# Two graph convolutions in one kernel: the groups of spans counted from the end, so that the last group is whole and serves block 48 alone

## The chip, the cores and the metric

The kernel runs on one core of a Trainium2 chip. The metric is device time in microseconds of one execution. The kernel before took 2149.52 us (median of 3 runs, 2146.58 to 2150.33).

Engines are named as in the profile: PE is TensorE, DVE is VectorE, ACT is ScalarE, POOL is GpSimd, SP is SyncE. PE multiplies, POOL issues the gathers (indirect DMAs, one row of 512 floats for each of 128 partitions), SP issues the plain DMAs, DVE and ACT do the elementwise work and take results out of PSUM.

## The reference

A graph of 6250 nodes and 100000 edges, sorted by destination; 512 features a node, all in float32. Cut to what matters:

```python
h = relu(layernorm(x))
dinv = where(deg > 0, rsqrt(max(deg, 1)), 0)          # deg counts src
norm = -dinv[src] * dinv[dst]
def conv(x, W0, W1, b):
    tx1 = segment_sum(x[src] * norm[:, None], dst)      # the propagation
    return x @ W0 + tx1 @ W1 + b
h = layer_norm(conv(h, W1_0, W1_1, b1)) * gamma + beta
h = where(h >= 0, h, 0.01 * h)
return x + conv(h, W2_0, W2_1, b2)
```

So there are two layers. Each gathers 100000 rows of 2 KB (x[src]), sums them by destination node, and multiplies 6250 x 512 by two 512 x 512 matrices. The second layer's gathers read what the first layer has written, from any node.

## The kernel before, in words

**Units of work.** The nodes are 49 *blocks* of 128 (block 48 has 106). The edges are 782 *chunks* of 128 in order of destination. A gather (L382, in `gather_to`) fetches one chunk, 128 rows, into one of 57 slots of the tile `places`, which are used in turn. A *span* (in the code a unit, `NU` = 261 of them) is a run of 32 consecutive nodes, of which it uses the first ones: span u begins at the node where chunk 3u begins, about 24 nodes after the span before it, and sums chunks 3u to 3u+3. Four spans make a *group*, 66 groups (`NS`). Before the change, groups are counted from the front: group g has spans 4g to 4g+3, and the last group, 65, has one span with two chunks, 780 and 781.

**What is done with a group.** `sums(g)` first builds `sel` on DVE (L465 and L474): for each span and chunk a 128 x 32 matrix of ones where an edge belongs to a node of the span. Then each product (L480) multiplies such a matrix by a gathered chunk and adds into one of four column quarters of the array, `ps[q * 32 : q * 32 + 32]`: quarter q holds span q of the group. The loop's outer index is the chunk's place in the span (`SPAN` = 4), the inner one the span, so that neighbouring products are in different quarters. ACT takes the 128 x 512 result out of PSUM as `agg[g]` (L483).

**What is done with a block.** A block is *due* when the last group that overlaps it is complete. `inside[i]` lists the groups that may overlap block i, with a margin of `DRIFT` = 32 nodes on either side for the uncertainty of where a group begins. Then:

- `turn(layer, i)` issues SP's loads for block i+2, transposes the block's own rows (`own`, L451, result taken out by ACT at L453), and *places* the groups' sums (`place`): for each group in `inside[i]`, DVE builds a 0/1 matrix `there` (L493) and PE does four products (L496) that both transpose the sums and shift them to the block's nodes. DVE scales the result into `aT` (L548).
- `dense(layer, i, ...)` multiplies the transposed own rows by W0 and `aT` by W1 (L458, four products each), and `finish` does the rest on DVE and ACT: in layer 0 bias (L511), layer norm, leaky relu, and two stores, to `tab[1]` (L527, which layer 1 gathers from) and `h_tab` (L532); in layer 1 bias (L506), the addition of x (L507) and the store of the output.

**Order.** PE, POOL and SP execute in the order in which the code issues (`manual_schedule`); DVE and ACT are put in order by a scheduler. For each layer the loop runs over the groups g: issue gathers as far as slots allow; `turn` for each block that is due (its last group is before g); `sums(g)`; then `dense` for those blocks. At g = NS - 2, the last group but one, the code does not wait for the next round: it does every block that doesn't need the last group (`turn` and `dense` of block 47), then for block 48 everything that can be done without the last group: its own transposes, its first products, and the placement of all its groups but the last. Then comes `sums(65)`, the last placement, the second products of block 48 and `finish`.

**Start.** Before the first group, the kernel computes degrees, the statistics of the first layer norm, the table of normalised rows (`make_table`, stored to `tab[0]`) and, for the first 60 chunks, which are gathered from x directly, scales each row after the gather (`find`, `look_up`, L407, L422 and L433). L326 spreads the first node of each span over the partitions (`row_ps`), from which `node_of` comes (L334 to L336).

**Check.** At g = 33 of layer 0, `check` counts violations of what the layout assumes: that the edges are sorted, that no span covers more than 32 nodes, and that each group begins within `DRIFT` nodes of its mean place. If the count is not zero, a second, general algorithm runs after this one.

Of the kernel before, what the change touches and what calls it, by code (L numbers as in the profile page):

```python
# [12 lines left out]
OP = mybir.AluOpType  # L13
# [6 lines left out]
P = 128  # L20
# [4 lines left out]
Q = 32  # L25
NQ = P // Q
STEP = 3
SPAN = STEP + 1
DRIFT = 32
# [10 lines left out]
def gnn_kernel(  # L40
# [45 lines left out]
    NS = -(-NU // NQ)  # L86
    rows = [min(P, N - i * P) for i in range(NB)]
# [216 lines left out]
    with tc.tile_pool(name="turn", bufs=1) as wp, tc.tile_pool(  # L304
# [18 lines left out]
        for k in range(2):  # L323
            for q in range(NQ):
                at = STEP * (q + k)
                nc.tensor.matmul(row_ps[q * Q : (q + 1) * Q, k, :], last.to_broadcast([P, Q]),  # L326
                                 dlx[:, at : at + STEP * NQ * (NS - 1) + 1 : STEP * NQ], start=True, stop=True)
# [27 lines left out]
def usual_path(tc, have):  # L355
    nc = tc.nc
    (x, out, tab, h_tab, ndinv_d, sidx, dlx, iota_r, w_sb, W2_1, W2_0, w_late, ident, eps, ones, first, node_of, minus,
     unsorted, ln, dinv, sdinv, bias1, bias2, gam, bet, unseen, N, E, D, NB, NC, NU, NS, KD, rows, places, order,
     groups, xs, sc, pick, src_lo, src_hi, p_id, dup) = (
        have[n] for n in ("x out tab h_tab ndinv_d sidx dlx iota_r w_sb W2_1 W2_0 w_late ident eps ones first node_of "  # L360
                          "minus unsorted ln dinv sdinv bias1 bias2 gam bet unseen N E D NB NC NU NS KD rows places "
# [4 lines left out]
    GN = NQ * STEP * P * N / E  # L366
    inside = [range(max(0, math.floor((i * P - DRIFT) / GN)), min(NS, math.ceil((i * P + r + DRIFT) / GN)))
              for i, r in enumerate(rows)]
    with ExitStack() as es:
# [6 lines left out]
        def zr(t):  # L376
            return places[:, order[t % R], :]
# [83 lines left out]
        def sums(g):  # L461

            n = min(NQ, NU - NQ * g)
            node = pool.tile([P, NQ, Q], F32, name="node")
            nc.vector.tensor_tensor(node[:, :n, :], first[:, NQ * g : NQ * g + n, None].to_broadcast([P, n, Q]),  # L465
                                    iota_r[:, None, 1 : Q + 1].to_broadcast([P, n, Q]), op=OP.add)
            sel = pool.tile([P, NQ, SPAN, Q], F32, name="sel")
            chunk = [range(STEP * (NQ * g + q), min(STEP * (NQ * g + q) + SPAN, NC)) for q in range(n)]
            same = n if len(chunk[-1]) == SPAN else 1
            for q in range(0, n, same):  # L470
                w = len(chunk[q])
                of = dlx[:, 1 + chunk[q][0] : 2 + chunk[q][0]]
                of = bass.AP(tensor=of.tensor, offset=of.offset, ap=[of.ap[0], [STEP, same], [1, w], [0, Q]])
                nc.vector.tensor_tensor(sel[:, q : q + same, :w, :], of,  # L474
                                        node[:, q : q + same, None, :].to_broadcast([P, same, w, Q]), op=OP.is_equal)
            ps = psum.tile([P, D], F32, name="ps")
            for s in range(SPAN):
                for q in range(n):
                    if s < len(chunk[q]):
# [508 lines left out]
```

## Time and profile before

| what | value |
|---|---|
| median of 3 runs (lowest, highest) | 2149.52 us (2146.58, 2150.33) |
| profiled execution, its own time | 2148.89 us |
| its span, first to last instruction | 2146.7 us |
| PE, POOL busy | 84%, 71% |
| DVE, ACT busy | 31%, 18% |
| granted PE clock, mean | 0.926 |
| DMA | 527.05 MB, 246 GB/s over the span |
| gathers from the tables (L382) | 1504, 0.96 us each |
| layer 0's last gather issued | 1087.69 us |
| layer 1's first gather issued | 1123.74 us |
| layer 1's last gather issued | 2109.66 us |

A row of the costliest groups gives the line, the engine, the operation, tiles, shape and count, then the busy time in us and the mean of one in ns, and after the second bar the engine's idle time before these instructions and what ended most of it. A row of the timeline gives start and duration in us, engine, line and operation; "x24" says that 24 records that follow each other are shown as one, and the bracket gives the idle time before them. A product in float32 leaves two records on PE (two passes), so the four products of one placement are 8 passes. A row of the windows gives, for one stretch of time, its length and then busy time and count for PE, the weight loads, DVE, ACT and POOL, the granted clock, the DMA engines' share and GB/s.

### The profile page before, as it was taken

Reading aid. Unit: us, or ns where it says so; the run is one execution under the profiler, and the core shown is the slowest. Engines: PE = TensorE matmul, PEld = TensorE weight load, DVE = VectorE, ACT = ScalarE, POOL = GpSimd, SP = SyncE. Lnnn points to the kernel's source line nnn. Section 1 sums busy time; section 2 is a strip of 40 time slices with the busy share of each in tenths; the row PEclk is TensorE's granted clock in tenths of the full one; section 3 lists DMA queues with packets and bytes.
Section 4 is the critical chain, followed back from the end, with each engine's and each line's share of the span. In section 5 each row is a group of like instructions: output and inputs, shape, how many; then the busy total and the mean of one; then the engine's idle time right before and its main releaser. Section 6 shows DMA issues by size and latency. Waiting matters only on the chain.

```text
span 2146.7 us, 23527 instructions
## 1 busy us (share of the span) xinstructions
PE 1795.7 (84%) x8843; PEld 794.7 (37%) x8843; DVE 674.8 (31%) x1341; ACT 382.7 (18%) x694; POOL 1520.2 (71%) x1577
## 2 busy tenths in 40 slices
PE   5669888988879888988876888889888888889888
PEld 4534333333334333433331333334333333334333
DVE  8974323333334233333330212212212212211211
ACT  7774212111112122111110000000000000000000
POOL 5067777777777777777727777777777777777772
PEclk9779999999989999999997989999999999999989
DMA  9298888788788888788837788888878888877883
GB/s 368 82 354 264 247 254 254 242 250 255 243 286 249 253 255 250 240 255 244 254 121 229 243 251 256 255 251 245 256 243 255 243 251 257 256 248 247 245 252 117
DMA packets 198945, 527.05 MB, mean 246 GB/s; under 512 B 31864, under 2 KB 46019, under 8 KB 198822
## 3 DMA queue, kind: packets, MB, share of 16 engines
q0 software_dynamic: 125120, 410.09, 62.4%
q1 hardware_dynamic: 73702, 115.36, 15.5%
q8 instruction: 71, 1.16, 0.2%
q14 instruction: 52, 0.43, 0.1%
HBM read 474.06 MB, written 51.27 MB: 245 GB/s over the span
## 4 chain that ended last, share of the span: by engine, by line
PE 48%; DMA 29%; POOL 9%; issue 8%; DVE 5%; ACT 0%; POOLq 0%; SPq 0%; ACTq 0%; DVEq 0%
DMA places<-tab,sidx 28%; PE u_ps L458 25%; PE ps L480 15%; POOL places L382 9%; PE aT_ps L496 5%; PE hT_ps L451 1%; DVE hi L252 1%; DVE lo L252 1%; DVE places L393 0%; PE both_ps L258 0%; DMA places<-in_x_dram,sidx 0%; DVE places L394 0%; PE u_ps L422 0%; PE hT_ps L422 0%; DVE both L428 0%
## 5 line engine op out<-in xcount | busy, mean ns | idle before, releaser
L382 POOL DMA_INDIRECT places<-tab,sidx x1504 | 1444.5, 960 | 493.8 <-issue 315.8
L480 PE MATMUL ps<-places,sel 128*32 128x512 f32 x4168 | 732.4, 666 | 280.7 <-DMA places<-tab,sidx 268.1
L480 PEld LDWEIGHTS ps<-places,sel 128*32 128x32 f32 x4168 | 141.8, 117 | 781.0 <-DMA places<-tab,sidx 591.3
L474 DVE TENSOR_TENSOR sel<-dlx,node 128x512 f32<-128x512 f32 x132 | 90.9, 688 | 750.0 <-PE ps L480 750.0
L496 PE MATMUL aT_ps<-there,agg 128*128 128x128 f32 (+2 forms) x2080 | 253.8, 278 | 1.4 <-ACT agg L483 1.4
L496 PEld LDWEIGHTS aT_ps<-there,agg 128*128 128x128 f32 (+1 forms) x2080 | 246.1, 196 | 4.2 <-ACT agg L483 3.2
L483 ACT ACTIVATE agg<-ps 128x512 f32<-128x512 f32 x132 | 78.8, 597 | 918.9 <-PE ps L480 918.9
L458 PE MATMUL u_ps<-places,hT 128*128 128x512 f32 (+1 forms) x392 | 185.8, 618 | 0.7 <-ACT hT L453 0.7
L458 PE MATMUL u_ps<-w,hT 128*128 128x512 f32 (+1 forms) x392 | 181.1, 605 | 0.7 <-ACT hT L453 0.7
L458 PE MATMUL u_ps<-places,aT 128*128 128x512 f32 (+1 forms) x392 | 178.0, 597 | 0.7 <-DVE aT L548 0.7
L458 PE MATMUL u_ps<-w,aT 128*128 128x512 f32 (+1 forms) x392 | 176.3, 592 | 0.7 <-DVE aT L548 0.7
L506 DVE TENSOR_TENSOR u_ps<-u_ps,bias 128x512 f32<-128x512 f32 x48 | 33.6, 700 | 294.9 <-PE u_ps L458 294.9
L511 DVE TENSOR_TENSOR u_ps<-u_ps,bias 128x512 f32<-128x512 f32 (+1 forms) x49 | 34.3, 700 | 284.3 <-PE u_ps L458 284.3
L453 ACT ACTIVATE hT<-hT_ps 128x512 f32<-128x512 f32 (+1 forms) x98 | 58.3, 595 | 349.6 <-PE hT_ps L451 348.2
L458 PEld LDWEIGHTS u_ps<-places,hT 128*128 128x128 f32 (+1 forms) x392 | 72.3, 195 | 117.3 <-issue 116.5
L458 PEld LDWEIGHTS u_ps<-w,hT 128*128 128x128 f32 (+1 forms) x392 | 70.3, 189 | 109.0 <-issue 106.5
L458 PEld LDWEIGHTS u_ps<-places,aT 128*128 128x128 f32 (+1 forms) x392 | 74.8, 191 | 95.4 <-issue 94.6
L458 PEld LDWEIGHTS u_ps<-w,aT 128*128 128x128 f32 (+1 forms) x392 | 74.3, 190 | 94.3 <-issue 93.4
L382 POOL DMA_INDIRECT places<-in_x_dram,sidx x44 | 45.0, 1024 | 86.8 <-ACT places L396 57.7
L448 ACT ACTIVATE h<-h,ln 128x512 f32<-128x512 f32 (+1 forms) x49 | 39.7, 813 | 283.3 <-DMA h<-in_x_dram 283.3
L493 DVE TENSOR_SCALAR there<-iota_r,node_of 128x128 f32<-128x128 f32 x260 | 76.6, 295 | 38.7 <-PE aT_ps L496 38.6
L548 DVE TENSOR_TENSOR aT<-aT_ps,to 128x512 f32<-128x512 f32 (+1 forms) x98 | 67.1, 685 | 39.4 <-PE aT_ps L496 37.9
(128 smaller groups left out, 942.7 us busy)
## 6 DMA issues: line engine op xcount, KB each, us to landing
places<-tab,sidx POOLq DMA_INDIRECT x1504
h<-in_x_dram SPq DMA_DIRECT2D x48, 256.0 KB
tab<-t SPq DMA_DIRECT2D x48, 256.0 KB
h_tab<-g SPq DMA_DIRECT2D x48, 256.0 KB
h<-h_tab SPq DMA_DIRECT2D x48, 256.0 KB
xt<-in_x_dram SPq DMA_DIRECT2D x48, 256.0 KB
out_dram<-t SPq DMA_DIRECT2D x48, 256.0 KB
places<-in_x_dram SPq DMA_DIRECT2D x4, 1792.0 KB
```

The costliest lines, as they stand in the source:

```text
L252: nc.vector.tensor_tensor(t, s[:, g * 2 * GJ : (g + 1) * 2 * GJ].rearrange("p (j s) -> p j s", s=2)[:, :, None, :] .to_broadcast([EP, GJ, ...
L382: nc.gpsimd.indirect_dma_start(out=zr(t), out_offset=None, in_=x if layer == 0 and t < RAW else tab[layer], in_offset=bass.IndirectOffsetO ...
L448: nc.scalar.activation(h[:r], h[:r], AF.Relu, bias=ln[:r, 1, i : i + 1], scale=ln[:r, 0, i : i + 1])
L453: nc.scalar.activation(hT[:, :, :r], ps[:, :, :r], AF.Copy)
L458: nc.tensor.matmul(u_ps[:r], hT[:, kc, :r], w[:, kc, :], start=(start and kc == 0), stop=(not start and kc == KD - 1))
L474: nc.vector.tensor_tensor(sel[:, q : q + same, :w, :], of, node[:, q : q + same, None, :].to_broadcast([P, same, w, Q]), op=OP.is_equal)
L480: nc.tensor.matmul(ps[q * Q : (q + 1) * Q, :], sel[:, q, s, :], zr(chunk[q][s]), start=(s == 0), stop=(s == len(chunk[q]) - 1))
L483: nc.scalar.activation(agg[g][: n * Q], ps[: n * Q], AF.Copy)
L493: nc.vector.tensor_scalar(there[:m, :r], iota_r[:m, :r], node_of[:m, g : g + 1], -(1.0 + i * P), op0=OP.subtract, op1=OP.is_equal)
L496: nc.tensor.matmul(placed[i][:, kc, :r], agg[g][:m, kc * P : (kc + 1) * P], there[:m, :r], start=(g == inside[i][0] and kc == 0), stop=(g ...
L511: nc.vector.tensor_add(v, v, bias1[:r])
L548: nc.vector.tensor_tensor(aT[:, :, :r], placed.pop(i)[:, :, :r], to.pop(i)[:, None, :r].to_broadcast([P, KD, r]), op=OP.mult)
```

## The change

Groups are counted from the end. `unit[g]` is the first span of group g: group 0 has one span (chunks 0 to 3), each other group four, and the last group has spans 257 to 260, chunks 771 to 781, fourteen products. Its mean first node is 6168, and block 48 begins at 6144; with a margin of 24 nodes for this limit in place of 32, group 65 overlaps block 48 alone. The list `inside` is computed from the mean limits and a margin for each, and `check` tests the tighter margin too.

`sums` is split: `choose` builds the selection on DVE, `sums` does the products and the eviction. For the last group `choose` is called ahead of block 47's `turn`. The last group's products are put in order of their chunks, so that products of the same span, which share a column quarter, mostly follow each other: quarters 0 0 0 1 0 1 1 2 1 2 2 3 2 3. Block 48's bias in layer 0 is added by a product of a row of ones with the bias on PE, among its first products, and no longer by DVE. In the start, L326 becomes two products for each of the eight before: one for group 0, one for the others.

```diff
+    unit = [max(0, NU - NQ * (NS - g)) for g in range(NS + 1)]
...
             for q in range(NQ):
-                at = STEP * (q + k)
-                nc.tensor.matmul(row_ps[q * Q : (q + 1) * Q, k, :], last.to_broadcast([P, Q]),
-                                 dlx[:, at : at + STEP * NQ * (NS - 1) + 1 : STEP * NQ], start=True, stop=True)
+                for g, n in ((0, 1), (1, NS - 1)):
+                    at = STEP * (unit[g] + q + k)
+                    nc.tensor.matmul(row_ps[q * Q : (q + 1) * Q, k, g : g + n], last.to_broadcast([P, Q]),
+                                     dlx[:, at : at + STEP * NQ * (n - 1) + 1 : STEP * NQ], start=True, stop=True)
...
-    GN = NQ * STEP * P * N / E
-    inside = [range(max(0, math.floor((i * P - DRIFT) / GN)), min(NS, math.ceil((i * P + r + DRIFT) / GN)))
-              for i, r in enumerate(rows)]
+    UN = STEP * P * N / E
+    mean = [UN * u for u in unit[:NS]] + [N]
+    drift = [0] + [DRIFT] * (NS - 2) + [min(DRIFT, int(mean[NS - 1]) - (NB - 1) * P), 0]
+    assert drift[NS - 1] >= Q // 2
+    inside = []
+    for i, r in enumerate(rows):
+        some = [g for g in range(NS) if mean[g] - drift[g] < i * P + r and mean[g + 1] + drift[g + 1] > i * P]
+        inside.append(range(some[0], some[-1] + 1))
...
-        def sums(g):
+        def choose(g):
...
+            return sel, chunk
+
+        def sums(g, sel, chunk):
+
+            n = len(chunk)
             ps = psum.tile([P, D], F32, name="ps")
-            for s in range(SPAN):
-                for q in range(n):
-                    if s < len(chunk[q]):
-                        nc.tensor.matmul(ps[q * Q : (q + 1) * Q, :], sel[:, q, s, :], zr(chunk[q][s]), start=(s == 0),
-                                         stop=(s == len(chunk[q]) - 1))
+            todo = [(s, q) for s in range(SPAN) for q in range(n) if s < len(chunk[q])]
+            if g == NS - 1:
+                todo.sort(key=lambda t: chunk[t[1]][t[0]])
+            for s, q in todo:
+                nc.tensor.matmul(ps[q * Q : (q + 1) * Q, :], sel[:, q, s, :], zr(chunk[q][s]), start=(s == 0),
+                                 stop=(s == len(chunk[q]) - 1))
...
-            nc.vector.tensor_add(v, v, bias1[:r])
+            if i < NB - 1:
+                nc.vector.tensor_add(v, v, bias1[:r])
...
+            m = NS - 1
+            nc.vector.scalar_tensor_tensor(of[:, :m], iota_r[0:1, :m], -NQ * UN, first[0:1, unit[1] : NU : NQ],
+                                           op0=OP.mult, op1=OP.add)
+            nc.vector.tensor_scalar_add(of[:, :m], of[:, :m], -mean[1])
+            nc.vector.tensor_mul(of[:, :m], of[:, :m], of[:, :m])
+            count(of[:, :m], OP.is_gt, float(DRIFT * DRIFT))
+            count(of[:, m - 1 : m], OP.is_gt, float(drift[m] * drift[m]))
...
-                    gather_to(layer, STEP * NQ * g + R)
+                    gather_to(layer, STEP * unit[g] + R)
...
-                sums(g)
+                sums(g, *(chosen if g == NS - 1 else choose(g)))
...
                 if g == NS - 2:
+                    chosen = choose(NS - 1)
                     while inside[i].stop < NS:
                         dense(layer, i, *turn(layer, i))
...
                     products(started[i], last_hT[layer], w_late[:, 1] if layer else w_sb[1], rows[i], True)
+                    if layer == 0:
+                        nc.tensor.matmul(started[i][: rows[i]], ones[0:1, : rows[i]], bias1[0:1, :], start=False,
+                                         stop=False)
                     place(i, inside[i][:-1])
```

## The prediction

> **What bounds the kernel now.** I read the page first, then the waits, then the two layer ends in the timeline.
>
> ```profile
> PE 1795.7 (84%) x8843; PEld 794.7 (37%) x8843; DVE 674.8 (31%) x1341; ACT 382.7 (18%) x694; POOL 1520.2 (71%) x1577
> ...
> L382 POOL DMA_INDIRECT places<-tab,sidx x1504 | 1444.5, 960 | 493.8 <-issue 315.8
> L480 PE MATMUL ps<-places,sel 128*32 128x512 f32 x4168 | 732.4, 666 | 280.7 <-DMA places<-tab,sidx 268.1
> ```
>
> PE looks busiest, yet it is PE that waits: 268.1 us for gathers (L480), while POOL's idle before a gather is mostly "issue", 0.30 us each. A window of layer 1 and the list of waits settle it:
>
> ```profile
> 1300.00:1500.00 200.00, 172.06 (x835) 74.61 (x833) 40.23 (x82) 13.73 (x23) 151.84 (x159) 0.97 0.81 251
> ...
> POOL places L382 <- DMA tab<-t: 35.1, 1, 35.1
> ```
>
> The fifth busy time is POOL's: 159 gathers in 200 us. One gather is 0.95 busy plus 0.30, so 1.253 us, back to back, without a real wait; 782 chunks make 980 us a layer, and no work on another engine shortens that. Once the gathers run, POOL's only long wait is the 35.1 us at the layer boundary, where layer 1's first gather needs layer 0's last table rows. So the time is: start, 782 gathers, tail, 782 gathers, tail. The change can only win or lose in the tails (and at the start). The tail of layer 0, on POOL and PE:
>
> ```profile
> 1087.69 0.95 POOL L382 DMA_INDIRECT places<-tab,sidx  x1 [0.30 <-issue]
> ...
> 1089.01 2.14 PE L480 MATMUL ps<-places,sel 128*32 128x512 f32 x10 [0.29 <-DMA places<-tab,sidx]
> 1091.08 0.66 PE L451 MATMUL hT_ps<-ident,h 128*128 128x128 f32 x4
> 1091.57 2.84 PE L496 MATMUL aT_ps<-there,agg 128*128 128x128 f32 x24
> 1094.25 3.60 PE L458 MATMUL u_ps<-w,hT 128*128 128x512 f32 x8
> 1101.12 0.53 PE L451 MATMUL hT_ps<-ident,h 106*128 106x106 f32 x4
> 1102.32 3.68 PE L458 MATMUL u_ps<-w,hT 128*106 128x512 f32 x8 [0.68 <-ACT hT L453]
> 1105.84 1.93 PE L496 MATMUL aT_ps<-there,agg 128*128 128x106 f32 x16
> 1107.70 1.90 PE L480 MATMUL ps<-places,sel 128*32 128x512 f32 x4
> 1109.64 0.59 ACT L483 ACTIVATE agg<-ps 32x512 f32<-32x512 f32 x1 [2.88 <-PE ps L480]
> ...
> 1115.83 0.70 DVE L511 TENSOR_TENSOR u_ps<-u_ps,bias 106x512 f32<-106x512 f32 x1 [3.58 <-PE u_ps L458]
> ...
> 1123.74 0.94 POOL L382 DMA_INDIRECT places<-tab,sidx  x1 [35.10 <-DMA tab<-t]
> ```
>
> After the last gather is issued (1087.69) PE still does all of block 47 and the first half of block 48 before group 65's two chunks; their sums leave PSUM 21.95 us after that issue (1109.64), and POOL resumes at 1123.74. Layer 1 repeats it: last issue 2109.66, eviction of the sums at 2131.58, 21.92 us.
>
> **The change, part by part.** Start-to-start on PE from those rows: transposes (own) 0.49; a placement (8 passes at 0.112) 0.89; a block's products 6.87; own of 48 with its wait 1.20; first products of 48 3.52; two placements and the switch to sums 1.86; sums of two chunks until the eviction 1.94. They add to 18.56 from 1091.08.
>
> *Moved: where group 64 ends.* Before, its last chunk is 780; after, 771, nine gathers earlier, 9 x 1.253 = 11.28 us. So PE is through with group 64 at 1079.80 instead of 1091.08. PE is in time for it: a group with a block due costs 3.6 (own and three placements) + 3.6 (sums) + 6.6 (products), 13.8 us, against 15.04 us for twelve gathers.
>
> *Added behind it.* Block 46 now falls due with group 64 (it was 63), so its 6.87 us of products stand behind these sums, in the tail. The chain until group 65's eviction: products of 46 6.87, own 0.49, two placements for 47 instead of three 1.79, products of 47 6.87, own of 48 1.20, its products 3.52, one placement instead of two 0.97, then X for the fourteen products of group 65. Without X: 21.71 us. All eleven chunks have landed by then (a gather lands about 3.7 us after its issue: chunk 780 was issued at 1086.43 and used at 1090.10), so no product waits for its chunk, in whatever order they stand; PE's own backlog is what is late next.
>
> *X, the unknown.* One product is two passes, and in one column quarter passes start 0.43 apart: the two chunks of one quarter above took four, 1.90. A whole group with quarters alternating does 32 passes in 3.64 us: four run side by side. By chunk, neighbours mostly share a quarter. If PE fills quarters independently, the longest has four products, 8 x 0.43 + 0.22 = 3.66 us. If a product in another quarter can start only after those ahead of it have started, quarters overlap only at their seams, sixteen passes deep: 16 x 0.43 + 0.22 = 7.1 us. If nothing overlaps, 28 x 0.43 + 0.22 = 12.3 us.
>
> ```profile
> 2098.31 3.64 PE L480 MATMUL ps<-places,sel 128*32 128x512 f32 x32
> ...
> 87.50:87.55 0.05, 0.03 (x2) 0.03 (x2) 1.00 0.00 0
> ```
>
> The Trainium skill (TensorE: Matmul & The Clock Gate, Part 3, The mechanism) speaks against the change: weight loads may be pulled ahead, but matmuls start and end in program order. Strictly so, a quarter's second pass (0.43 later) would hold the next quarter back, and 16 products would take 16 x 0.43 = 6.9 us and more; the first row has 3.64. The second row looks at L282, where both two-pass products of one column half stand before those of the other: two matmuls start within 0.05 us, 0.013 apart in the single records (87.519, 87.532), so the second half did not wait for the first. That looks past seven instructions; group 65 needs ten or more. By the rule X is 7.1, by the rows 3.66. I take 3.66.
>
> *Layer 1:* 21.71 + 3.66 = 25.37 from 2113.01 - 11.28 = 2101.73, so 2127.1 against 2131.58: 4.5 us won. The rest (eviction 0.6, a placement with 128 rows instead of 32, four products, final add) has the same instructions.
>
> *Layer 0:* the bias product adds two passes, 0.86, and a switch of the array's tiling, about 0.1; 26.33 from 1079.80 gives 1106.1 against 1109.64: 3.5 us. It removes L511 on block 48, 0.70 + 0.03 on the path, so 4.2 us earlier at POOL.
>
> *Start.* L326 issues 16 products, not 8: sixteen more passes, four side by side each 0.117 us, 0.47. The evictions after it gate L407, hence the look-ups and the table of group 2 that POOL waits for (first unbroken gather 125.66). DVE idles 0.77, 0.66 and 0.59 before that, so 0 to 0.5; I take 0.5 lost.
>
> *Placements.* Counting which groups each block overlaps gives 145 a layer instead of 130 (three for nearly every block, as the groups' limits fall): 30 x 0.95 = 28.5 us more PE work, with 15 more DVE tiles (0.29) a layer. Outside the tails it lies in PE's waits for gathers (125.1 us in the last 900 us); without that cover all 28.5 us would count.
>
> *At nothing:* the last selection is built early (DVE 0.7, some 20 us before use); gathers are released nine chunks later, but PE trails POOL by under 4 us of landing while 57 slots give some 45 gathers (56 us) of lead, so no slot is waited for; the check's five small DVE operations fall at group 33, where no block is due; SP's stores of 46 and 47 come earlier or stay ahead of their readers.
>
> *Sum:* 4.5 + 4.2 - 0.5 = 8.2 us. The profiled execution took 2148.89 (span 2146.7 and 2.2 around it), so 2140.7; it lies 0.6 under the median 2149.52, so for a median **2141**.
>
> **Rivals.** (1) *Program order holds* (X = 7.1): each tail loses 3.4 of its gain, 8.2 - 6.9 = 1.3 us left, 2148, no change. For it the skill's rule, against it L282 and the 32-pass row. Part of the way (a window of a few instructions, X 4.5 to 5.5) gives 2143 to 2145. (2) *Slower:* the fourteen products run one after the other in both layers' last groups, X = 12.3: 8.6 lost twice, 8.2 - 17.2 = -9.0, 2158.5. The turn is X of about 7.8 us. Against it: quarters in different products do overlap. (3) *Placements on the path:* PE falls behind gathers and 28.5 us show: 2170. It needs over 15.04 us a group; rows make 13.8, so only a much lower clock would do it. (4) *The change doesn't do what it says:* the check counts a group's first node too far off and the second algorithm runs as well. The inputs' largest drift is 19 nodes against 32, the last 1 against 24; I give it nothing.
>
> **How the numbers follow.** What a measurement here can tell from no change is about 0.2%, 4.3 us. Quarters independent 0.62 (2137 to 2143); part of the way 0.14, at 2143 to 2146, about half of it beyond the 4.3 us; program order 0.10; slower 0.14, for (2), (3) and what I don't see. Faster 0.70, same 0.16, slower 0.14. The clock adds 1.7 either way: the last products took 3.68 in layer 0, but 5.38 in layer 1 (2134.04), where four of eight passes ran at half speed; either tail can fall either way. The range, **2137 to 2149**, takes the likeliest with that and the cases up to program order, and leaves out the slower ones.
>
> **What would show it.** Right: the last gather of layer 0 still starts near 1088 and POOL's long wait shrinks from 35.1 to about 31 us; group 65's 28 passes take about 3.7 us; the step from last issue to their eviction is 18.4 in layer 0 and 17.4 in layer 1; gathers still 1.253 apart. Wrong: those 28 passes take 7 or 12 us; PE's idle before them shows a wait for chunks or the selection; or POOL shows waits for sums, the sign that PE has become the bound.

## The result, and the profile after

The changed kernel takes 2138.46 us (median of 9 runs, 2133.50 to 2141.23), the kernel before 2147.34 us (9 runs beside them, 2142.04 to 2150.33). The ratio is 0.9959, 95% interval 0.9945 to 0.9973: 8.9 us less, between 5.8 and 11.8. The profiled execution took 2138.41 us, span 2136.5, against 2148.89 and 2146.7.

From the page of the changed kernel, its busy times and the two groups that answer to L382 and L480 (now L389 and L495):

```profile
PE 1794.0 (84%) x9101; PEld 815.3 (38%) x9101; DVE 683.5 (32%) x1375; ACT 384.2 (18%) x694; POOL 1515.0 (71%) x1577
...
L389 POOL DMA_INDIRECT places<-tab,sidx x1504 | 1439.9, 957 | 491.0 <-issue 316.2
L495 PE MATMUL ps<-places,sel 128*32 128x512 f32 x4168 | 713.3, 660 | 266.4 <-DMA places<-tab,sidx 253.6
```

PE has 258 matmuls more and waits 14.5 us less for gathers (268.1 before). Its busy time did not grow (1795.7 before): the placements' rows take 26 us more (253.8 at L496, now 279.9 at L511), but the sums' rows, as many as before, take 19 us less (732.4 to 713.3), with a granted clock of 0.935 against 0.926. The stretch of layer 1 that was shown of before, and POOL's long wait:

```profile
1300.00:1500.00 200.00, 174.87 (x872) 76.59 (x874) 42.10 (x88) 13.74 (x23) 151.88 (x159) 0.97 0.80 251
...
POOL places L389 <- DMA tab<-t: 33.1, 1, 33.1
```

Still 159 gathers in 200 us: POOL bounds the kernel as it did. Its wait between the layers went from 35.1 to 33.1 us, where I had said about 31. The end of layer 0, in order of time:

```profile
1075.76 3.70 PE L465 MATMUL u_ps<-w,hT 128*128 128x512 f32 x8
...
1083.54 0.94 POOL L389 DMA_INDIRECT places<-tab,sidx  x1 [0.30 <-PE hT_ps L458]
1084.96 3.60 PE L465 MATMUL u_ps<-w,hT 128*128 128x512 f32 x8
...
1093.03 3.68 PE L465 MATMUL u_ps<-w,hT 128*106 128x512 f32 x8 [0.68 <-ACT hT L460]
1096.64 1.10 PE L685 MATMUL u_ps<-bias,ones 1*106 1x512 f32 x2
1097.67 1.14 PE L511 MATMUL aT_ps<-there,agg 128*128 128x106 f32 x8
1098.74 5.40 PE L495 MATMUL ps<-places,sel 128*32 128x512 f32 x28
1104.22 0.60 ACT L498 ACTIVATE agg<-ps 128x512 f32<-128x512 f32 x1 [6.76 <-PE ps L495]
...
1117.61 0.94 POOL L389 DMA_INDIRECT places<-tab,sidx  x1 [33.12 <-DMA tab<-t]
```

The order is the one forecast: group 64's sums end before the last gather is even issued (the first row starts behind them), block 46's products follow, then all of block 47, block 48's first products, the bias product, one placement, and the 28 passes X of the last group. No row of PE waits for a gather. But X takes 5.40 us, which is neither 3.66 nor 7.1. The sums leave PSUM 20.68 us after the last issue (1104.22 - 1083.54; 18.4 forecast, 21.95 before). Layer 1 has the same 5.40, and the eviction 21.07 us after the last issue (17.4 forecast, 21.92 before).

Where the 10.2 us between the two spans lie, by POOL's gathers (unbroken ones are issued without a wait):

| stretch | before | after | difference |
|---|---|---|---|
| until the first unbroken gather | 125.66 | 125.25 | -0.4 |
| gathers of layer 0, to the last issue | 962.03 | 958.29 | -3.7 |
| last issue of layer 0 to first of layer 1 | 36.05 | 34.07 | -2.0 |
| gathers of layer 1, to the last issue | 985.92 | 984.60 | -1.3 |
| last issue to the end | 37.05 | 34.31 | -2.7 |

The tails, from which I expected 8.7 us, give 4.7 here, and 1.7 of that are the last products of layer 1, which took 5.38 us before and 3.68 after. Five lie in the stretches of gathers, some 4 of them in the pace: one gather is busy for 0.949 us in most cases before and 0.946 after, and the unbroken ones start 1.253 and 1.250 us apart. So the total was right, and two things needed explaining: why X is 5.40, and what the gathers and the missing 4 us are.

### The profile page after: what moved, and what is told of

Its sections match the earlier page's. It is cut to its first block, busy times and chain, and to the rows that moved or that the text cites. A ratio compares the mean times of both kernels' runs of the same rounds, so it can differ in the third digit from the quotient of the medians.

```text
span 2136.5 us, 24099 instructions
## 1 busy us (share of the span) xinstructions
PE 1794.0 (84%) x9101; PEld 815.3 (38%) x9101; DVE 683.5 (32%) x1375; ACT 384.2 (18%) x694; POOL 1515.0 (71%) x1577
## 4 chain that ended last, share of the span: by engine, by line
PE 51%; DMA 28%; POOL 10%; issue 7%; DVE 4%; ACT 0%; POOLq 0%; SPq 0%; ACTq 0%
DMA places<-tab,sidx 27%; PE u_ps L465 25%; PE ps L495 16%; POOL places L389 10%; PE aT_ps L511 6%; PE hT_ps L458 1%; DVE lo L253 1%; DVE hi L253 1%; DMA places<-in_x_dram,sidx 0%; PE both_ps L259 0%; PE hT_ps L429 0%; DMA h<-in_x_dram 0%; DVE places L400 0%; PE u_ps L429 0%; DVE both L435 0%
## 5 line engine op out<-in xcount | busy, mean ns | idle before, releaser
L389 POOL DMA_INDIRECT places<-tab,sidx x1504 | 1439.9, 957 | 491.0 <-issue 316.2
L495 PE MATMUL ps<-places,sel 128*32 128x512 f32 x4168 | 713.3, 660 | 266.4 <-DMA places<-tab,sidx 253.6
L495 PEld LDWEIGHTS ps<-places,sel 128*32 128x32 f32 x4168 | 142.5, 116 | 748.8 <-DMA places<-tab,sidx 536.3
L483 DVE TENSOR_TENSOR sel<-dlx,node 128x512 f32<-128x512 f32 (+3 forms) x134 | 90.9, 679 | 712.6 <-PE ps L495 712.6
L511 PE MATMUL aT_ps<-there,agg 128*128 128x128 f32 (+2 forms) x2320 | 279.9, 277 | 1.5 <-ACT agg L498 1.5
L511 PEld LDWEIGHTS aT_ps<-there,agg 128*128 128x128 f32 (+1 forms) x2320 | 271.3, 194 | 5.1 <-ACT agg L498 3.3
L498 ACT ACTIVATE agg<-ps 128x512 f32<-128x512 f32 (+1 forms) x132 | 78.7, 597 | 904.6 <-PE ps L495 904.6
L521 DVE TENSOR_TENSOR u_ps<-u_ps,bias 128x512 f32<-128x512 f32 x48 | 33.6, 699 | 295.1 <-PE u_ps L465 295.1
L527 DVE TENSOR_TENSOR u_ps<-u_ps,bias 128x512 f32<-128x512 f32 x48 | 33.6, 700 | 291.4 <-PE u_ps L465 291.4
L389 POOL DMA_INDIRECT places<-in_x_dram,sidx x44 | 44.6, 1013 | 87.3 <-ACT places L403 57.6
L508 DVE TENSOR_SCALAR there<-iota_r,node_of 128x128 f32<-128x128 f32 (+1 forms) x290 | 83.7, 289 | 42.0 <-PE aT_ps L511 42.0
```

What stands on the lines that cost most here:

```text
L389: nc.gpsimd.indirect_dma_start(out=zr(t), out_offset=None, in_=x if layer == 0 and t < RAW else tab[layer], in_offset=bass.IndirectOffsetO ...
L483: nc.vector.tensor_tensor(sel[:, q : q + k, :w, :], of, node[:, q : q + k, None, :].to_broadcast([P, k, w, Q]), op=OP.is_equal)
L495: nc.tensor.matmul(ps[q * Q : (q + 1) * Q, :], sel[:, q, s, :], zr(chunk[q][s]), start=(s == 0), stop=(s == len(chunk[q]) - 1))
L498: nc.scalar.activation(agg[g][: n * Q], ps[: n * Q], AF.Copy)
L508: nc.vector.tensor_scalar(there[:m, :r], iota_r[:m, :r], node_of[:m, g : g + 1], -(1.0 + i * P), op0=OP.subtract, op1=OP.is_equal)
L511: nc.tensor.matmul(placed[i][:, kc, :r], agg[g][:m, kc * P : (kc + 1) * P], there[:m, :r], start=(g == inside[i][0] and kc == 0), stop=(g ...
```

## The experiments

### X: how PE hands out passes

The starts of the single passes of X, read from the trace of the changed kernel, are these: quarter 0 starts at 1098.745, quarter 1 at 1099.634, quarter 2 at 1100.522, quarter 3 at 1101.410, each 0.89 us or two passes behind the one before. From it I formed **theory W**: passes are handed out in program order, and a column quarter holds four, one that runs and three that wait; a pass for a full quarter holds up every pass behind it, also those for idle quarters. Its rivals were strict program order, a price for every change of quarter, and (later) **theory N**, a price for each pair of neighbours in the same quarter.

The first four runs went together to another chip, on which the kernel before took 2550.91 us (2541.04 to 2557.24, 30 runs). What is different there comes below; X can be read on any chip. The changed kernel again, and two other orders of the fourteen products, first quarters 0 1 2 3 in turn, then all of a quarter before the next:

```diff
             todo = [(s, q) for s in range(SPAN) for q in range(n) if s < len(chunk[q])]
-            if g == NS - 1:
-                todo.sort(key=lambda t: chunk[t[1]][t[0]])
```

```diff
-                todo.sort(key=lambda t: chunk[t[1]][t[0]])
+                todo.sort(key=lambda t: t[1])
```

> The changed kernel, unchanged, beside the control. Theory A: the two tails and the start alone win, by the two profiles so far 2.0 us at the layer boundary, 0.9 until the last sums of layer 1 are evicted, up to 1.7 from the clock in the last products, 0.4 at the start: 3 to 5 us, ratio 0.9977 to 0.9985. Theory B, gathers faster as well: 8 to 9 us, ratio 0.9955 to 0.9963. Both expect the 28 passes of the last group at 5.4 us.

> The changed kernel with the last group's products in the order of the other groups, quarters 0 1 2 3 in turn. Theory W, a column quarter holds four passes (one running, three waiting) and passes are handed out in program order, so that by chunk the second, third and fourth quarter start late by 0.89, 1.78 and 2.67 us: here the 28 passes take 3.4 to 3.7 us instead of 5.4, both tails are 1.8 us shorter, 3.5 us in all less than the changed kernel. Rival, the order by chunk saves waiting for the last chunks: the row is no shorter and shows a wait for a gather, the time is the same or longer.

> The changed kernel with the last group's products sorted by quarter: four of quarter 0, four of 1, four of 2, two of 3. Theory W: the next quarter starts when the fifth of the eight passes before it starts, four passes or 1.72 us later each time, so the fourth starts 5.15 us after the first and the row takes 16 passes, 6.9 us plus 0.2; each tail 1.5 us longer than in the changed kernel, 3.0 us in all. Rival, matmuls start in program order: the next quarter starts with the last of eight passes, 3.0 us later each time, 10.7 us. Rival, quarters independent: 3.5 us. Nothing overlaps: 12 us.

The rows of X in layer 1's end, from the three timelines in that order:

```profile
2522.33 5.40 PE L495 MATMUL ps<-places,sel 128*32 128x512 f32 x28
```

```profile
2521.23 3.63 PE L493 MATMUL ps<-places,sel 128*32 128x512 f32 x28
```

```profile
2524.02 7.14 PE L495 MATMUL ps<-places,sel 128*32 128x512 f32 x28
```

Layer 0 has the same three numbers. Quarter by quarter, the four quarters start 1.75 us apart (2524.017, 2525.764, 2527.511, 2529.257), which is four passes: eight passes are due in the first quarter, four fit, and the next quarter starts when the last of the eight is taken. W fits all three. The times (ratios to the kernel before: 0.9972 [0.9959, 0.9985] as changed, 0.9950 [0.9932, 0.9967] in turn, 0.9983 [0.9968, 0.9998] by quarter) stand in the same order; the step of 3.5 us that X makes in two layers is near what their intervals can tell apart.

N fits too, with 1.77 us for four such neighbours and 3.5 for ten, so a further order was made for which the two disagree: two products of a quarter, then two of the next.

```diff
-                todo.sort(key=lambda t: chunk[t[1]][t[0]])
+                todo.sort(key=lambda t: (t[0] // 2, t[1]))
```

> The changed kernel with the last group's products in another order: two products of the first quarter, two of the second, two of the third, two of the fourth, and then two of each again. Theory W (passes are handed out in program order and a quarter of the columns holds four, one that runs and three that wait): two products are four passes, so no quarter ever holds the others up, and the twenty-eight passes take 3.6 us as in quarters 0 1 2 3 in turn. Theory N (each pair of neighbours in the same quarter costs a pass or nearly: 1.77 us for the four such pairs of the order by chunk, 3.5 us for the ten of the order by quarter, so 0.35 to 0.44 us for each): seven such pairs, 6.1 to 6.7 us. Time: by W 1.8 us less in each layer than the changed kernel, 3.5 us in all; by N 1.4 to 2.6 us more.

```profile
1100.46 3.67 PE L495 MATMUL ps<-places,sel 128*32 128x512 f32 x28
```

3.67 us in layer 0, 3.66 in layer 1: N falls, W stands. Two products are four passes, exactly what a quarter holds, and all four quarters start within 0.04 us. (Every product here is two passes, so these runs don't tell "four passes" from "two products".) This run and those that follow were on chips where the kernel before takes 2147 to 2148 us: 2134.52 us, ratio 0.9941 [0.9918, 0.9963].

### The gathers' pace: both kernels on one chip again

> The kernel before, once more, for a profile beside the others of this set. Theory A (a gather's time on POOL belongs to the chip and the execution, not to the kernel): the unbroken gathers are as far apart here as in the changed kernel of this set, 1.250 to 1.254 us for both, equal to within 0.001 us. Theory B (the change itself brings them from 1.253 to 1.250 us): 1.253 here and 1.250 in the changed kernel. If the chip is one on which POOL's gathers bound the kernel the time is 2140 to 2152 us and POOL's wait between the layers 35 us; if it is one on which TensorE is held back, as in the first set, 2545 to 2557 us and 76 us.

> The change as it was made. Where the gathers bound the kernel: the tails alone give 2.0 us between the layers, 0.9 behind the last gather and up to 1.7 by the clock of the last products, so under Theory A the ratio to the kernel before is 0.9975 to 0.9985 in spans once the gathers' pace is the same in both, and under Theory B 0.9955 to 0.9965. Where TensorE is held back: 0.996 to 0.9985 as in the first set. The twenty-eight passes of the last group take 5.40 us in both layers under every theory that is left.

The kernel before, against itself, 2144.93 us, ratio 0.9988 [0.9974, 1.0002]; the changed kernel beside it 2137.89 us, 0.9952 [0.9937, 0.9966], with X at 5.40 in both layers. The unbroken gathers are 1.2504 us apart in layer 0 of both, 1.2502 and 1.2504 in layer 1, and the stretches agree: 958.9 and 959.6 us in layer 0, 982.9 and 982.2 in layer 1. So theory A holds: 1.253 belonged to the one execution that was profiled first (or to its chip; this isn't told apart), and the change has no part in it. But the time is not what I wrote beside A. Span against span, 2147.1 and 2137.6, the tails gave 9.7 us: 3.2 between the layers (POOL's wait 36.8 to 33.6) and 6.5 behind the last gather (41.1 to 34.65). The execution of the kernel before that was profiled is the longest of its ten (2149.23 us; median 2144.93, and 2147.51 in the 17 runs beside them), so the pair may show more than is usual. The end of layer 1 in the kernel before, this time:

```profile
2105.94 0.95 POOL L382 DMA_INDIRECT places<-tab,sidx  x1 [0.30 <-issue]
2107.31 1.06 PE L480 MATMUL ps<-places,sel 128*32 128x512 f32 x8 [0.40 <-DMA places<-tab,sidx]
2111.23 1.91 PE L480 MATMUL ps<-places,sel 128*32 128x512 f32 x2 [2.86 <-DMA places<-tab,sidx]
2113.07 1.12 PE L451 MATMUL hT_ps<-ident,h 128*128 128x128 f32 x4
...
2132.15 0.59 ACT L483 ACTIVATE agg<-ps 32x512 f32<-32x512 f32 x1 [7.37 <-PE ps L480]
...
2134.61 5.38 PE L458 MATMUL u_ps<-places,aT 128*106 128x512 f32 x8 [0.69 <-DVE aT L548]
```

Group 64's last chunk, 780, arrives late: PE waits 2.86 us for it, and group 64 ends 7.2 us after the last issue, where the execution I had worked from had 3.4. All of that is on the chain of the kernel before. And the last products run about half their passes at half rate (5.38 us) in both layers, not in one. The changed kernel has neither here: group 64 ends 5.7 us before the last issue, chunks that land late have some 20 us of other work ahead of them, and its last products take 3.68.

### The grouping alone

The order in turn, and block 48's bias added by VectorE as before:

```diff
-            if g == NS - 1:
-                todo.sort(key=lambda t: chunk[t[1]][t[0]])
...
-            if i < NB - 1:
-                nc.vector.tensor_add(v, v, bias1[:r])
+            nc.vector.tensor_add(v, v, bias1[:r])
...
-                    if layer == 0:
-                        nc.tensor.matmul(started[i][: rows[i]], ones[0:1, : rows[i]], bias1[0:1, :], start=False,
-                                         stop=False)
```

> The grouping and block 48's place alone: the changed kernel with the last group's products in quarters 0 1 2 3 in turn, and with block 48's bias in layer 0 added by VectorE as before, without the bias product. The twenty-eight passes take 3.63 us. In layer 0 the 1.03 us that the bias product held the chain are gone and one addition of 0.73 us is back behind the last products, so that the wait of POOL between the layers is 0.3 us shorter than with the bias product and 2.0 to 2.1 us shorter than in the changed kernel. Where the gathers bound the kernel the time is 3.8 us below the changed kernel, ratio to the kernel before 0.992 to 0.995; where TensorE is held back the same 3.8 us, 0.994 to 0.997. The rival that the three parts belong together (grouping alone gives nothing, the order by chunk and the bias product earn it) would give 0.998 to 1.001.

2134.10 us, ratio 0.9939 [0.9923, 0.9956]; X 3.63 us, the eviction 18.5 and 18.6 us after the last issue, POOL's wait 31.6 us, 2.0 less than in the changed kernel of the set before. The grouping and block 48's place earn the whole gain. By the rows the other two parts take some of it back: the order by chunk 1.77 us a layer, the bias product 0.3 (1.03 us on PE's chain for the 0.73 of L511). The times point the same way (0.9939 here, 0.9952 as changed, on another chip), but their intervals overlap.

### The placements under the waits

Each of blocks 1 to 47 gets one more group placed, the one before its first; its rows fall outside the block and add zeros:

```diff
-        inside.append(range(some[0], some[-1] + 1))
+        inside.append(range(some[0] - (1 <= i < NB - 1), some[-1] + 1))
```

> The changed kernel with one more group placed for each of blocks 1 to 47 in both layers, the one before its first, whose rows all fall outside the block and add zeros: 94 more placements of 0.95 us, 89 us of PE and 94 comparisons of 0.3 us on VectorE; the output is the reference's. If placements lie under PE's waits for gathers (254 us in the changed kernel) where the gathers bound the kernel, only those of the last two blocks of each layer show, 1 to 2 us a layer behind the last gather: 2 to 5 us more than the changed kernel. If they were paid for, 89 us more, and by the same rule the 30 that the change adds would have cost 28 us. Between the two if the waits that have room are not where the placements fall: 20 to 50 us more. Where TensorE is held back and the gathers wait for it, 60 to 110 us more.

2145.86 us, ratio 0.9992 [0.9979, 1.0004], 7 to 8 us above the changed kernel of the other sets and not 2 to 5. PE's wait for gathers falls from about 252 us to 202.5; that wait, PE's busy time, and the rows of the sums and of the placements:

```profile
PE ps L495 <- DMA places<-tab,sidx: 202.5, 140, 13.4
...
PE 1847.2 (86%) x9853; PEld 894.0 (42%) x9853; DVE 712.8 (33%) x1469; ACT 384.1 (18%) x694; POOL 1517.3 (71%) x1577
...
L495 PE MATMUL ps<-places,sel 128*32 128x512 f32 x4168 | 687.9, 661 | 214.2 <-DMA places<-tab,sidx 202.5
L511 PE MATMUL aT_ps<-there,agg 128*128 128x128 f32 (+1 forms) x3072 | 360.9, 276 | 1.5 <-ACT agg L498 1.5
```

So of 89 us of added PE work some 81 are hidden and 8 show. The waits took only 50 of them. PE's busy time rose by no more than 51 us (1796.6 in the changed kernel of the set before), although the placements' rows grew by 83 (from 277.7): the sums' rows, as many as before, fell by 30 (from 717.8), and the granted clock rose from 0.930 to 0.943. Whether the sums got shorter by the clock or because more chunks lay ready when PE came to them wasn't taken apart. In the profiled execution 1.9 us of the added work lie behind the last gather (36.5 against 34.65), and up to 0.8 between the layers; it was the quickest of its ten runs (2142.38), and where the rest lies wasn't seen. Taken in proportion, the change's own 30 placements cost up to 2.5 us, an estimate from 8 x 30 / 94, where I had written nothing.

### The half rate in the last products

Five of six profiled layer ends of the kernel before have 5.38 us in the last products; with the change in any form it is one of 18 (layer 0 of the order by pairs). The Trainium skill (TensorE: Matmul & The Clock Gate, Part 1, What's actually happening) says that the clock halves after a window of about 3.4 us that counts as idle, and that the windows run free. Layer 0 of the kernel before, in the set on one chip, agrees: within the row below, the half rate lasts from 1110.756 to 1114.120, 3.4 us, and begins in the middle of the products.

```profile
1109.76 5.38 PE L458 MATMUL u_ps<-w,aT 128*106 128x512 f32 x8 [0.69 <-DVE aT L548]
```

What counts as idle was to be found with two edits of the kernel before: work in PE's two waits, or the last group's two products in all four quarters side by side (three write rows that nothing reads).

```diff
+        def fill():
+            idle = psum.tile([P, KD, P], F32, name="hT_ps")
+            for k in range(KD):
+                nc.tensor.transpose(idle[:, k, :], ident, ident)
...
+            if g == NS - 1:
+                fill()
             agg[g] = pool.tile([P, D], F32, name="agg", bufs=4)
...
+            if i == NB - 1:
+                fill()
             aT = pool.tile([P, KD, P], F32, name="aT", bufs=1)
```

```diff
-                        nc.tensor.matmul(ps[q * Q : (q + 1) * Q, :], sel[:, q, s, :], zr(chunk[q][s]), start=(s == 0),
-                                         stop=(s == len(chunk[q]) - 1))
+                        for k in [q] if g < NS - 1 else range(NQ):
+                            nc.tensor.matmul(ps[k * Q : (k + 1) * Q, :], sel[:, q, s, :], zr(chunk[q][s]),
+                                             start=(s == 0), stop=(s == len(chunk[q]) - 1))
```

> The kernel before, with TensorE kept busy in its two waits at each layer's end: four transposes of the identity (0.11 us a pass, into a PSUM tile that nothing reads) behind the last group's sums, where PE waits 0.68 us for their eviction, and four behind the last placement, where it waits 0.69 us for the scaled copy. In the kernel before, the last eight products took 5.38 us in five of six layer ends that were profiled, the first half of them at half rate, and 3.68 in one; in the kernels with the change 3.68 in 17 of 18. Theory G (the two waits between short runs of work let the rate drop): 3.68 us in both layers here, 1.7 us less in each, 2145.5 for a median of 2148 or so of the kernel before, ratio 0.998 to 0.999. Theory Q (it is the four passes in one quarter of the columns, and in 32 of the rows, that leave the array mostly idle, whatever the waits): 5.38 in both, ratio 1.000.

> The kernel before, with the last group's two products issued in all four quarters of the columns side by side (three of them into rows of the sums that nothing reads) instead of in the first alone: the row still takes 1.9 to 2.0 us, but fills the array. Theory Q (an array in which one quarter works counts as idle): the last eight products take 3.68 us in both layers, ratio 0.998 to 0.999. Theory G (the two waits let the rate drop): 5.38 in both layers as in the kernel before, ratio 1.000. If both runs show 3.68, either kind of work is enough; if both show 5.38, what keeps the rate up in the changed kernel is the length of its last group's sums, 3.6 to 7.1 us instead of 1.9.

Both have 3.68 us in both layers; the ends of layer 1:

```profile
2137.98 1.90 PE L485 MATMUL ps<-places,sel 128*32 128x512 f32 x4
2139.81 0.66 PE L464 MATMUL hT_ps<-ident 128*128 128x128 f32 x4
2140.56 1.14 PE L503 MATMUL aT_ps<-there,agg 32*128 32x106 f32 x8
2141.62 0.66 PE L464 MATMUL hT_ps<-ident 128*128 128x128 f32 x4
2142.39 3.68 PE L458 MATMUL u_ps<-places,aT 128*106 128x512 f32 x8
```

```profile
2134.87 1.92 PE L481 MATMUL ps<-places,sel 128*32 128x512 f32 x16
2137.50 1.14 PE L497 MATMUL aT_ps<-there,agg 32*128 32x106 f32 x8 [0.70 <-ACT agg L484]
2139.32 3.68 PE L458 MATMUL u_ps<-places,aT 128*106 128x512 f32 x8 [0.69 <-DVE aT L549]
```

In the second, the row lasts as long as before and the waits are as they were; only the array is fuller. By the rows, either kind of work is enough in these four layer ends. By the times nothing is won: 2146.59 us, ratio 1.0000 [0.9990, 1.0009], and 2149.56 us, 1.0005 [0.9993, 1.0017], where 0.998 to 0.999 was expected. Either the half rate is rarer in executions that are not profiled, or something that wasn't seen takes the gain back; so this stays open, and the 1.7 us a layer are not to be counted as shown in the times.

The two profiles do show group 64 ending late in layer 1 again, 6.1 and 5.8 us after the last issue. So of four profiles of this order on such chips, three end it 5.8 to 7.2 us after, and the one I worked from ends it at 3.4. But the three are of long executions: 2149.23, 2156.56 and 2153.05 us, the longest of ten, the longest of 13 and the second longest of 12. How often the chunk is late in the others isn't shown. In layer 0 all four have 3.4 to 3.5.

### A chip on which TensorE is held back

> The kernel before, unchanged, timed against itself: how far two executions of one program differ. Theory A, the gathers' pace is a property of the execution and not of the change (1.253 us a gather in the profile before, 1.250 in the profile after, some 4 us over 1500 gathers): this profile shows the pace that the changed kernel shows on the same chip, within 0.001 us, and the ratio to itself is 1.000 +- 0.001. Theory B, the change makes the gathers faster: 1.253 here again, 1.250 in the changed kernel beside it.

On the chip of the first four runs the kernel before took 2550.71 us, ratio to itself 1.0004 [0.9990, 1.0018]. Some of the waits of POOL and of PE in that run (us in total, times, longest us; "remote" is a releaser that the profile can't name, and the last two rows are of time in which it names none):

```profile
POOL places L382 <- remote: 198.3, 90, 10.0
POOL places L382 <- PE ps L480: 113.2, 61, 15.4
...
PE aT_ps L496 <- issue: 227.0, 207, 10.3
PE ps L480 <- issue: 144.3, 174, 2.5
```

PE idles 371 us in two lines in which nothing that the profile shows holds it up; in the first profile these lines wait for gathers, selections or evictions, and 0.2 us for nothing named. Matmul starts in these stretches often lie 0.7, 1.4, 2.1 or 2.8 us apart, and once 10.7. The gathers are just as fast (1.2505 us apart while they run), but POOL now waits 113.2 us for PE's sums (30.3 in the first profile) and 198.3 for what has no name, and group 64's sums end 42 us after the last gather's issue. The chain there is 62% PE. What holds PE back wasn't found; it isn't the change, since both kernels and both layers show it. All runs on that chip were of one set, so the chip is the likely seat of it, but it wasn't visited again. The change gave 0.9972 there, and by another way than on the other chips: seen from the last gather its tail is longer (76.0 to 78.6 us), while the last gathers of the two layers are issued 7.6 and 11.1 us earlier. Which of PE's stalls became fewer wasn't taken apart.

### A version that beats both

The order in turn, and block 48's own transposes, its first products and the bias product moved from the tail to behind group 61, in which no block falls due and PE waits for gathers. Its rows get their own SBUF tile, loaded two groups earlier, and its products the eighth PSUM bank (the new helper for that load and the order of the products are left out here):

```diff
+                if g == NS - 7:
+                    load_h(layer, NB - 1)
+                if g == NS - 5:
+                    last_hT[layer] = own(layer, NB - 1)
+                    u_last = started[NB - 1] = psum.tile([P, D], F32, name="u_last", bufs=1)
+                    products(u_last, last_hT[layer], w_late[:, 1] if layer else w_sb[1], rows[NB - 1], True)
+                    if layer == 0:
+                        nc.tensor.matmul(u_last[: rows[NB - 1]], ones[0:1, : rows[NB - 1]], bias1[0:1, :],
+                                         start=False, stop=False)
                 if g == NS - 2:
...
-                    last_hT[layer] = own(layer, i)
-                    started[i] = psum.tile([P, D], F32, name="u_ps")
-                    products(started[i], last_hT[layer], w_late[:, 1] if layer else w_sb[1], rows[i], True)
```

> The changed kernel with the last group's products in the order of quarters 0 1 2 3, and with block 48's own transposes, its products with its own rows and the bias product issued behind group 61, in which no block falls due, with a buffer and a PSUM bank of their own, instead of behind blocks 47's products. Where the gathers bound the kernel (PE waits for gathers at group 61 and has the time): the tail loses 0.53 + 0.67 + 3.68 us in both layers, 1.03 us more in layer 0, and 1.77 us of the last group's passes: 7.7 us in layer 0 and 6.7 in layer 1, some 14 us less than the changed kernel, ratio to the kernel before 0.988 to 0.991. Rival: the moved work delays group 61's sums and with them the gathers, or the last gather's landing (9.3 us behind its issue at the earliest point at which the sums could start) now ends the chain: half of that or less, 0.992 to 0.995. Where TensorE is held back and some five groups behind the gathers, moved work is not hidden: only the passes' 1.77 us and the 0.67 us wait in each layer are saved, 4.9 us, ratio 0.994 to 0.996.

2124.26 us (2123.55 to 2126.73), ratio 0.9891 [0.9866, 0.9917]: 13.6 us below the changed kernel beside it, where 14 were expected. The end of layer 0:

```profile
1091.36 3.60 PE L470 MATMUL u_ps<-w,aT 128*128 128x512 f32 x8
1094.80 1.03 PE L514 MATMUL aT_ps<-there,agg 128*128 128x106 f32 x8
1095.76 3.63 PE L498 MATMUL ps<-places,sel 128*32 128x512 f32 x28
```

Between block 47's products and X one placement is left, and X still starts without a wait for a chunk, 9.2 us after the last issue (1086.59). The eviction follows 12.9 us after it in layer 0 and 14.4 in layer 1, POOL's wait is 25.4 us, and the gathers' stretches (959.8 and 981.4 us) are those of the other kernels. This is also the clearest evidence for the bound: work that leaves the tail is free elsewhere.

## Why the prediction was right, and where it was not

The time, 2141 forecast and 2138.46 measured, was right, and so was "faster". Not all of its steps were, and that the total came out so near is in part luck: one step was 3.5 us too good, and terms that had been put at nothing or left open seem to have given about as much back.

**The bound.** POOL's gathers bound both kernels, and only the ends of the layers count: shown by the stretches of gathers, the same within some 2 us in the four kernels that ran beside each other on one chip, and by the version that moved work out of the tail.

**Where group 64 ends.** Forecast 11.28 us earlier. In layer 0 of the two first profiles it ends 3.46 us after the last issue before, and 7.71 before it after: 11.17. Right. In layer 1 it was 9.5, from +3.42 to -6.09: PE came to it late, since it had waited for the last chunk of the group before, 759, which was issued at 2074.70 and used only 6.6 us later.

```profile
2081.32 1.04 PE L495 MATMUL ps<-places,sel 128*32 128x512 f32 x2 [1.54 <-DMA places<-tab,sidx]
...
2092.48 3.64 PE L495 MATMUL ps<-places,sel 128*32 128x512 f32 x32
```

**The chain without X.** Forecast 21.71, with the bias product 22.67. From the end of group 64's sums to the start of X: 21.7 in layer 1, 22.9 in layer 0. Right.

**X.** "I take 3.66" is the step that failed: 5.40. The rows it was taken from were read rightly, but they could not tell independent quarters from a window of four passes: the 32-pass row goes round the quarters, and L282 puts four passes ahead of the next half, which is just what fits. The rival "part of the way", 4.5 to 5.5, had named the size and had 0.14; the time that was put beside it, 2143 to 2146, did not come. The measurement also decides between the row and the rule of the Trainium skill (TensorE: Matmul & The Clock Gate, Part 3, The mechanism): in the changed kernel quarter 1's first pass starts at 1099.634, and three passes of quarter 0 that stand before it in the code start after it, the last at 1100.915. So strict order of starts doesn't hold here; order comes in only through a full quarter. The price was 1.74 us in each layer, 3.5 in all, and with it the sum 8.2 becomes 4.7. That the tails of the first two profiles give 4.7 as well is chance: 1.7 of it is the rate of the last products of layer 1, where the sums were evicted only 0.85 us earlier against the last issue (21.92 to 21.07) and not 2.7, as group 64 ended 1.8 us later than forecast.

**What made it good again, as far as is known.** Two terms that I had from one execution. "The rest has the same instructions" took group 64's last chunk to be there 3.4 us after the last issue, as in the profile; in three of four profiles of that order it is 5.8 to 7.2 in layer 1, on the chain before and off it after. Averaged over those four, the eviction in layer 1 is 24.7 us after the last issue, and 21.25 over the two profiles of the changed kernel on such chips: 3.4 won, which may be too much for a usual execution, as the three were long ones. In layer 0 it is 22.0 and 20.9: 1.1, and L511's 0.7 on top. That makes 5.2, just below the interval of 5.8 to 11.8. The other term is the rate of the last products, which I had let fall "either way": in the profiles it falls against the kernel before in three of four layer ends on such chips and never against the change as it was made, up to 1.7 us each; with 1.7 for layer 1 and half of it for layer 0 the sum is 7.8. That this part is in the times as well wasn't confirmed, so 3.7 of the 8.9 us stay open.

**The bias product** costs 1.03 (forecast 0.96) and saves 0.73: right, and a loss. **The start:** 0.5 us lost forecast; 0.2 lost in the pair on one chip. **The placements:** hidden, but for up to 2.5 of 28.5 us by the estimate above, and only in part where I had put them: PE's waits for gathers fell by 14.5 us, the sums' rows by 19. **Program order and the slower rival** fell with X; "PE falls behind the gathers" is what the first chip of the experiments is like, but in both kernels.

## What to carry to other kernels

Passes for different column quarters run side by side only as far as the order of issue lets them: go round the quarters, with at most what one quarter holds (here four passes, two float32 products) before the next. In a kernel that one queue bounds, cost only what stands behind that queue's last item, and move everything that doesn't need that item to where the other engines wait. A chain that starts at a transfer's landing should be costed from several executions, since one profile can show a landing that others don't.

## What the runs showed of the hardware that I had not expected

- A column quarter of TensorE holds four passes of 128x512 float32 (two products), one that runs and three that wait. 28 passes took 3.63 us in turn, 3.67 in twos, 5.40 by chunk and 7.14 by quarter; 0.43 us is one pass, and the starts of the quarters (0.89 and 1.75 us apart) are two and four passes.
- On one chip the same kernel took 19% longer (2551 us, 2147 elsewhere) with gathers of the same pace: TensorE idled 371 us in two lines without a cause that the profile names, its matmuls often 0.7, 1.4, 2.1 or 2.8 us apart.
- 89 us more of placements raised TensorE's busy time by only 51 us (1796.6 to 1847.2): the sums' rows fell by 30, with a granted clock of 0.943 against 0.930.
- A gather's busy time, 0.949 us in one execution and 0.946 in all others, makes about 4 us over 1500 of them: as much as half of what this change is worth.
